# Normalised input laid out with features in rows: loaded turned from DRAM and normalised in place, in place of transposes on TensorE

## The chip, the cores and the metric

The kernel runs on one core of one Trainium2 chip. The metric is the device time of one execution in microseconds; the time before is the median of three runs. A core has engines with a queue each, which work in order and wait for each other by semaphores: PE (TensorE, matrix products into PSUM), DVE (VectorE), ACT (ScalarE), POOL (GpSimd) and SP, which here issues DMAs. PEld is PE's loading of weights.

## The reference

A residual block on x of 8 sequences of 512 tokens with 256 features: layer norm, then windowed attention (16 heads of 16, each token sees the last 250) and a gated feed-forward net with weights of +1 and -1, multiplied.

```python
def _layernorm(x, axis=-1, eps=1e-05):
    m = jnp.mean(x, axis=axis, keepdims=True)
    v = jnp.var(x, axis=axis, keepdims=True)
    return (x - m) / jnp.sqrt(v + eps)
...
    x = L0_attn_query
    xn = _layernorm(x, axis=-1)
    s = _L0_attn_ref(xn, L0_attn_in_proj_w, L0_attn_out_proj_w)
    g = _silu(_L0_ffn_ref(xn, L0_ffn_k0, L0_ffn_k1, L0_ffn_k2, L0_ffn_s0, L0_ffn_s1, L0_ffn_s2))
    x = x + s * g
```

In attention q, k and v are xn times the rows of in_proj_w, q and k are rotated by position, and softmax runs over the window. In the net, h = relu(s0 * [xn, -xn] @ w0) * 2, h = relu(s1 * h @ w1) * 2, h = s2 * h @ w2, with 1024 hidden columns twice.

## The kernel before

**Layout.** A sequence is four tiles of 128 tokens (rows) by 256 features. Layer norm wants tokens in rows, so that mean and variance run along a row; the products of q, k, v and the net want features in rows, because PE contracts over rows. So each tile is normalised (`norm`, DVE, line 250) and then turned by PE: `turn_x` (line 268) multiplies two 128x128 blocks by an identity into PSUM (`xnT_ps`). From PSUM come three things: `xT` in fp32 (DVE line 280, ACT line 278 for sequence 0), its high part `xh` in fp16 with a factor of 128 and the sign of s0 (ACT, line 281), and the rest `xl` (DVE, line 284). The net runs over high and low parts, so each product is done twice (`layer`, line 415: h1 from x in 8 column blocks, h2 from h1 in 8; `last`, line 441: z).

**Stages of a sequence b.** `stats` (DVE, with the power -1/2 on POOL, line 240), `norm`, `turn_x`, then `project` (PE, line 307: ka, kb, qa, qb, the even and odd members of the rotation pairs), times cos and sin on DVE (line 319), `rotate` on POOL (line 339), splits into two parts (ACT 356, DVE 363), a trip through DRAM that stacks heads (`to_dram`, `stack`, on SP), `scores`, exponentials (ACT 624), masks (POOL 640 and 647), `values` into po, divisions, `project_o` (line 782), the product with the gate, and the residual. `project_v` (line 292) is done at the start of the sequence itself. Preparation of sequence b+1 runs beside the net and the attention of b.

**Order.** All of it is written as pieces (time, cost, function) and one function `run` sorts them by time and calls them; a piece can return followers with a delay. The times are the planner's own, in which a sequence is SEQ = 42 long, against some 75 us on the chip; they set nothing but the order of instructions in the engines' queues. The order among engines is kept by semaphores.

**Buffers.** `one` holds a single xT, xh and xl. PSUM pool `ps_m` has three banks in rotation for h, z, q/k/v, att and xnT; `ps_s` two for scores, `ps_o` one for values. `turned` holds m_ka, m_kb and their like: tag `ma` twice, tag `mb` once. `work` holds two each of xn, den and xr.

**Start and end.** While the first x is loaded and normalised, `warm` has PE multiply the identity 16 times. The weights w1 arrive as bytes and are turned to +1 and -1 with a scale by POOL (line 180) and ACT (line 178), block by block, among other work. In the last sequence h2 runs in two halves of 256 tokens, and for its tiles 2 and 3 `project_o` comes before `last`: att goes to SBUF on ACT (line 791) and the end (lines 450 to 464) is exponential, plus 1, reciprocal, product and sum on DVE, then the store.

```python
at = dict(stats=9 if b > 1 else 12, norm=14.5, x=16.5, k=22, q=25, v=SEQ + 0.6)
...
out += [
    (at["norm"] + dx * t, 0, lambda t=t: norm(b, t)),
    (at["x"] + dx * t, 0.25, lambda t=t: turn_x(b, t, plain)),
    (at["v"] + dv * t, 0.87, lambda t=t: project_v(b, t)),
]
```

Of the kernel before, what the change touches and what calls it, by code (L numbers as in the profile page):

```python
# [11 lines left out]
F32 = mybir.dt.float32  # L12
F32R = mybir.dt.float32r
# [21 lines left out]
def tile_attention_times_gated_ffn(  # L35
    ctx: ExitStack,
    tc: tile.TileContext,
    x: bass.AP,
    w_qkv: bass.AP,
    w_o: bass.AP,  # L40
    k0: bass.AP,
# [3 lines left out]
    rope: bass.AP,  # L45
    out: bass.AP,
):

# [152 lines left out]

    quick = set()

    def warm():

        pw = ps_m.tile([P, P], F32, tag="mm", name="warm")
        for n in range(16):
            nc.tensor.matmul(pw, ident, ident, start=(n == 0), stop=(n == 15))  # L210

    def run(pieces):
        clock, count_, due = 0.0, itertools.count(), []
# [17 lines left out]
    def stats(b):  # L231
        st = states[b] = {}
        mv = small.tile([P, NT, 2], F32, tag="mv", name=f"mv_{b}")
        rstd = small.tile([P, NT], F32, tag="rstd", name=f"rstd_{b}")
        for t in range(NT):
            bn = small.tile([P, 6], F32, tag="bn", name=f"bn_{b}_{t}")
            nc.vector.bn_stats(bn, xs[b, t])
            nc.vector.bn_aggr(mv[:, t, :], bn)
        nc.vector.tensor_scalar(rstd, mv[:, :, 1], EPS, None, ALU.add)
        nc.gpsimd.tensor_tensor(rstd, rstd, minus_half, ALU.pow)  # L240
        nc.vector.scalar_tensor_tensor(
            mv[:, :, 1], mv[:, :, 1], LEAST_VAR, ones, ALU.is_ge, ALU.mult,
            accum_out=counts[:, 2 * B + b : 2 * B + b + 1],
        )
        st["mv"], st["rstd"] = mv, rstd

    def norm(b, t):
        st = states[b]
        xn = st["xn", t] = work.tile([P, E], F32, tag="xn", name=f"xn_{b}_{t}")
        nc.vector.tensor_scalar(  # L250
            xn, xs[b, t], st["mv"][:, t, 0:1], st["rstd"][:, t : t + 1],
            ALU.subtract, ALU.mult,
        )

    def turn_x(b, t, plain=False):

        st = states[b]
        xn = st.pop(("xn", t))
        if t == 0:
            st["xT"] = one.tile([P, EC, T], F32, tag="xT", name=f"xT_{b}")  # L260
            if plain:
                st["xp"] = one.tile([P, EC, T], F32, tag="xl", name=f"xp_{b}")
            else:
                for p, dt in (("h", F16), ("l", F32R)):
                    st["x" + p] = one.tile([P, EC, T], dt, tag="x" + p, name=f"x{p}_{b}")
        pt = ps_m.tile([P, EC, P], F32, tag="mm", name=f"xnT_ps_{b}_{t}")
        for c in range(EC):
            nc.tensor.transpose(pt[:, c, :], xn[:, ts(c, P)], ident)  # L268
        if plain:
            nc.vector.tensor_copy(st["xT"][:, :, ts(t, P)], pt)  # L270
            nc.scalar.mul(st["xp"][:, :, ts(t, P)], pt, sgnx)
            return
        hi, lo = (st["x" + p][:, :, ts(t, P)] for p in "hl")

        def parts_():
            xT = st["xT"][:, :, ts(t, P)]
            if b == 0:
                nc.scalar.copy(xT, pt)
            else:
                nc.vector.tensor_copy(xT, pt)  # L280
            nc.scalar.mul(hi, pt, sgnx)

        def low():
            nc.vector.scalar_tensor_tensor(lo, pt, sgnx, hi, ALU.mult, ALU.subtract)

        return [(0.0, parts_), (0.5, low)]
# [15 lines left out]
    def project(b, what, part):  # L302
        st = states[b]
        col = E * "qk".index(what) + P * "ab".index(part)
        ps = ps_m.tile([P, T], F32, tag="mm", name=f"{what}{part}_ps_{b}")
        for c in range(EC):
            nc.tensor.matmul(  # L307
                ps, wqkv_sb[:, c, ds(col, P)], st["xT"][:, c, :],
                start=(c == 0), stop=(c == EC - 1),
            )  # L310

        m = turned.tile(
            [P, 2, T], F32, tag=f"m{part}", name=f"m_{what}{part}_{b}",
            bufs=2 if part == "a" else 1,
        )
        st[what, part] = m

        def times(i):
            nc.vector.tensor_tensor(  # L319
                m[:, i], ps, rope_sb[:, i if part == "a" else 1 - i], ALU.mult  # L320
            )

        def both():
            times(0)
            times(1)
            if part == "b":
                return [
                    (1.4, lambda: rotate(b, what)),
                    (4.0 if b else 7.0, lambda: split_hi(b, what)),
                    (5.1 if b else 8.2, lambda: split_lo(b, what)),  # L330
                ]

        return [(0.0, both)]
# [39 lines left out]

    def prepare(b, plain=False):

        if b == 0:
            at = dict(stats=-40, norm=-38, x=-36, k=0, q=3, v=9.2)
            dx, dp, dv = 1.0, 1.5, 1.5
        else:

            at = dict(stats=9 if b > 1 else 12, norm=14.5, x=16.5, k=22, q=25, v=SEQ + 0.6)
            dx, dp, dv = 1.5, 1.5, 1.0
            at = {n: SEQ * (b - 1) + f for n, f in at.items()}
        out = [(at["stats"], 0, lambda: stats(b))]
        for t in range(NT):
            out += [
                (at["norm"] + dx * t, 0, lambda t=t: norm(b, t)),
                (at["x"] + dx * t, 0.25, lambda t=t: turn_x(b, t, plain)),
                (at["v"] + dv * t, 0.87, lambda t=t: project_v(b, t)),
            ]  # L390
        for what in "kq":
            out += [
                (at[what], 1.75, lambda w=what: project(b, w, "a")),
                (at[what] + dp, 1.75, lambda w=what: project(b, w, "b")),
            ]
        return out
# [32 lines left out]
    def last(b, t, how):  # L429
# [16 lines left out]
        if how == "final":  # L446
            den = denominator(b, t)

            def ends():
                nc.scalar.activation(den, pz, AF.Exp, scale=scales[:, 1:2])  # L450
                nc.vector.scalar_tensor_tensor(
                    gate, pz, scales[:, 0:1], st["att", t], ALU.mult, ALU.mult
                )
                return [(0.5, add)]

            def add():
                nc.scalar.activation(den, den, AF.Identity, bias=1.0)
                return [(0.4, final)]

            def final():  # L460
                nc.vector.reciprocal(den, den)
                nc.vector.tensor_tensor(gate, gate, den, ALU.mult)
                nc.vector.tensor_tensor(gate, gate, st["xr", t], ALU.add)
                nc.sync.dma_start(out[b, ts(t, P), :], gate)

            return [(0.0, ends)]

        def scale():
            nc.vector.tensor_scalar(gate, pz, scales[:, 0:1], None, ALU.mult)
            if how != "later":  # L470
                return [(0.5, lambda: gate_ready(b, t))]

        return [(0.0, scale)]

# [45 lines left out]

    def late(b, t):

        if b + 1 == B:
            return SEQ * b + 40.0 + 0.9 * t
        return SEQ * (b + 1) + (32.0 + 3.2 * t if b + 2 < B else 18.0 + 2.5 * t)
# [194 lines left out]
    def attention(b, among):  # L720
# [16 lines left out]
            out.append((times[n], 1.7, lambda n=n: step(b, n)))  # L737
        for g in range(NG):

            at = times[used[g - 2][-1]] + 0.01 if g > 1 else first - (10.0 if b else 2.0)  # L740
            if b and g == 1:
                at = first + 0.01
            out.append((at, 0, lambda g=g: stack(b, g)))
# [34 lines left out]
    def project_o(b, t, final=False):  # L778
# [7 lines left out]
        xr = work.tile([P, E], F32, tag="xr", name=f"xr_{b}_{t}")  # L786
        nc.sync.dma_start(xr, x[b, ts(t, P), :])
        st["xr", t] = xr
        if final:
            att = st["att", t] = work.tile([P, E], F32, tag="xn", name=f"att_{b}_{t}")  # L790
            return [(0.0, lambda: nc.scalar.copy(att, pp))]

        def product():
            y = st["gate", t]
            nc.vector.tensor_tensor(y, pp, y, ALU.mult)
            return [(0.5, store)]

        def store():
            y = st.pop(("gate", t))
# [35 lines left out]
    def swap():  # L835
# [2 lines left out]
        outs = ctx.enter_context(tc.tile_pool(name="outs", bufs=1))  # L838

    everything = [  # L840
        (-38.5, 0, signs), (-40.5, 0, warm),
        (18.2, 0, make_w2), (22.5, 0, swap), (SEQ * (B - 1) + 45.0, 0, add_up),
    ]
    for c in range(EC):
        everything.append((-30 + 0.1 * c, 0, lambda c=c: make_w0(c)))
    for w, f, at, engine in (
        ("l", 0, -20, nc.gpsimd), ("l", 1, -19, nc.gpsimd), ("l", 2, -18, nc.gpsimd),
        ("h", 0, -17, nc.scalar), ("h", 1, -16, nc.scalar), ("h", 2, 5, nc.gpsimd),
        ("l", 3, 9.0, nc.gpsimd), ("l", 4, 9.1, nc.gpsimd), ("l", 5, 9.2, nc.gpsimd),
        ("l", 6, 9.3, nc.gpsimd), ("l", 7, 9.4, nc.gpsimd), ("h", 3, 15.2, nc.scalar),  # L850
        ("h", 4, 17.0, nc.scalar), ("h", 5, 18.7, nc.scalar), ("h", 6, 20.4, nc.scalar),
        ("h", 7, 22.2, nc.scalar),
    ):
        everything.append((at, 0, lambda f=f, w=w, e=engine: make_w1(f, w, e)))
# [139 lines left out]
```

## Time and profile before

| | us |
|---|---|
| median of 3 runs | 631.65 (629.59 to 631.93) |
| profiled execution | 632.4 |
| its span, first to last instruction | 630.6 |
| PE busy in it | 609.6 |
| DVE, POOL, ACT busy | 393.0, 316.1, 300.0 |
| transposes, PE, 64 of 285 ns (overlapping) | 12.8 |
| xn, xl, xT on DVE | 23.3, 15.1, 11.7 |
| xh on ACT | 15.3 |

The page lists busy time by engine and groups of instructions by line and tile. [...]sums of lengths overstate, and start to start is what counts. The mean granted TensorE clock was 0.993. Between the span and the execution's time lie 1.8 us.

### The profile page before, as it was taken

What the parts mean: (1) busy time and instruction counts of PE and PEld (TensorE: products, weight loads), DVE (VectorE), ACT (ScalarE), POOL (GpSimd) and SP (SyncE); (2) the same over time, 40 slices, a digit from 0 to 9 for tenths busy, and PEclk for the clock granted to TensorE, in tenths of its full rate; (3) what the DMA queues carried; (4) which work ended last, traced back from release to release, by engine and by line L of the source; (5) the groups of instructions that cost most, each with busy time, mean ns of one, the idle gap of its engine ahead of it and who ended that gap; (6) DMA issues with size and microseconds to landing.
All of it is one profiled execution on the core that took longest, in us unless ns stands there. A gap on an engine that the chain in (4) does not pass through costs nothing.

```text
span 630.6 us, 12029 instructions
## 1 busy us (share of the span) xinstructions
PE 609.6 (97%) x4834; PEld 398.8 (63%) x4834; DVE 393.0 (62%) x668; ACT 300.0 (48%) x442; POOL 316.1 (50%) x406
## 2 busy tenths in 40 slices
PE   7899999999999999999999999999999999999993
PEld 5454566656665567755676566765676556777883
DVE  6582545757656674766758576485675668457664
ACT  3566564525455445535355454453444544564421
POOL 1945452356623566327644367234662356638630
PEclk9899999999999999999999999999999999999998
DMA  8261821125321163113521153402532116230101
GB/s 269 81 234 51 300 86 50 36 83 210 101 76 50 68 223 112 51 51 144 166 93 51 55 221 96 132 25 94 207 107 73 51 68 226 76 109 18 53 26 40
DMA packets 38193, 67.20 MB, mean 107 GB/s; under 512 B 5104, under 2 KB 19184, under 8 KB 38128
## 3 DMA queue, kind: packets, MB, share of 16 engines
q1 hardware_dynamic: 36384, 64.24, 30.2%
q10 hardware_dynamic: 1744, 2.10, 1.0%
q8 instruction: 40, 0.66, 0.4%
q14 instruction: 25, 0.20, 0.1%
HBM read 36.96 MB, written 29.36 MB: 105 GB/s over the span
## 4 chain that ended last, share of the span: by engine, by line
PE 84%; DVE 6%; DMA 4%; POOL 3%; ACT 2%; issue 1%; SPq 0%; POOLq 0%; ACTq 0%
PE h_ps L415 40%; PE po L679 11%; PE z_ps L441 9%; PE sc L605 7%; PE v_ps L292 4%; PE att_ps L782 4%; PE qa_ps L307 2%; PE kb_ps L307 2%; PE qb_ps L307 2%; DMA kb<-in_k_dram 2%; DMA xr<-in_x_dram 2%; PE ka_ps L307 2%; PE xnT_ps L268 1%; DVE den L505 1%; ACT p L624 1%
## 5 line engine op out<-in xcount | busy, mean ns | idle before, releaser
L624 ACT ACTIVATE p<-sc 128x1024 f32<-128x1024 f32 (+2 forms) x144 | 138.5, 1013 | 75.0 <-PE sc L605 41.0
L640 POOL TENSOR_SCALAR_AFFINE_SELECT p<-p 128x512 f32<-128x512 f32 x128 | 93.8, 739 | 106.5 <-ACT p L624 106.5
L415 PE MATMUL h_ps<-h1l,w1l_sb 128*128 128x512 f32 (+1 forms) x576 | 144.2, 392 | 0.0
L415 PE MATMUL h_ps<-h1h,w1h_sb 128*128 128x512 f16 (+1 forms) x576 | 123.0, 356 | 0.9 <-ACT v_pad L299 0.5
L415 PEld LDWEIGHTS h_ps<-h1l,w1l_sb 128*128 128x128 f32 x576 | 99.5, 188 | 25.7 <-issue 6.8
L426 ACT ACTIVATE h2h<-h_ps 128x512 f16<-128x512 f32 (+1 forms) x72 | 39.6, 550 | 136.5 <-PE h_ps L415 136.4
L415 PEld LDWEIGHTS <-w1h_sb 128*128 128x128 f16 x576 | 51.6, 98 | 55.8 <-issue 14.0
L647 POOL TENSOR_SCALAR_AFFINE_SELECT p<-p 128x512 f32<-128x512 f32 (+1 forms) x96 | 50.4, 525 | 58.0 <-ACT p L624 56.7
L679 PE MATMUL po<-p,v_pad 128*32 128x378 f32 (+4 forms) x1216 | 77.0, 372 | 1.6 <-DVE S L703 1.1
L424 DVE SCALAR_TENSOR_TENSOR h2l<-h_ps,h2h 128x512 fp32r<-128x512 f32 (+1 forms) x72 | 44.4, 617 | 52.0 <-ACT h2h L426 52.0
L505 DVE RECIPROCAL den<-den 128x256 f32<-128x256 f32 x30 | 52.5, 1749 | 26.0 <-POOL den L501 26.0
L424 DVE SCALAR_TENSOR_TENSOR h1l<-h_ps,h1h 128x512 fp32r<-128x512 f32 x64 | 42.5, 675 | 36.1 <-ACT h1h L426 36.1
L605 PEld LDWEIGHTS sc<-q,k 32*128 32x128 f32 x1216 | 44.1, 184 | 26.1 <-issue 15.0
L754 DVE RECIPROCAL S<-S 128x128 f32<-128x128 f32 x64 | 58.9, 934 | 0.0
L426 ACT ACTIVATE h1h<-h_ps 128x512 f16<-128x512 f32 x64 | 38.2, 597 | 43.0 <-PE h_ps L415 42.8
L605 PE MATMUL sc<-q,k 32*128 32x378 f32 (+4 forms) x1216 | 57.3, 306 | 0.0
L415 PE MATMUL h_ps<-xl,w0l_sb 128*128 128x512 f32 x128 | 53.6, 500 | 0.0
L679 PEld LDWEIGHTS po<-p,v_pad 128*32 128x32 f32 x1216 | 31.5, 109 | 30.8 <-issue 16.6
L800 POOL TENSOR_TENSOR gate<-gate,xr 128x256 f32<-128x256 f32 x30 | 23.1, 770 | 46.7 <-DMA xr<-in_x_dram 32.6
L415 PE MATMUL h_ps<-xh,w0h_sb 128*128 128x512 f16 x128 | 39.5, 391 | 0.1
L441 PE MATMUL z_ps<-w2l_sb,h2l 128*128 128x256 f32 x256 | 38.1, 291 | 0.0
L339 POOL TENSOR_TENSOR m_ka<-m_ka,m_kb 128x512 f32<-128x512 f32 x16 | 20.1, 1276 | 30.3 <-DVE m_kb L319 30.3
(95 smaller groups left out, 806.6 us busy)
## 6 DMA issues: line engine op xcount, KB each, us to landing
q<-dq SPq DMA_DIRECT2D x64, 256.0 KB, 3.5
dq<-qh SPq DMA_DIRECT2D x16, 512.0 KB, 3.4
dq<-m_qa SPq DMA_DIRECT2D x16, 512.0 KB, 4.6
k<-dk SPq DMA_DIRECT2D x32, 256.0 KB, 2.8
dk<-kh SPq DMA_DIRECT2D x8, 512.0 KB, 2.7
dk<-m_ka SPq DMA_DIRECT2D x8, 512.0 KB, 2.7
xr<-in_x_dram SPq DMA_DIRECT2D x32, 128.0 KB, 2.3
out_dram<-gate SPq DMA_DIRECT2D x32, 128.0 KB, 1.7
```

Source lines behind the costliest of these rows:

```text
L307: nc.tensor.matmul(ps, wqkv_sb[:, c, ds(col, P)], st["xT"][:, c, :], start=(c == 0), stop=(c == EC - 1),)
L415: nc.tensor.matmul(ph, w[p][:, c, ts(f, P)], st[src + p][:, c, cols], start=(k == 0), stop=(k == n - 1),)
L424: nc.vector.scalar_tensor_tensor(lo, ph, 0.0, hi, ALU.max, ALU.subtract)
L426: high = lambda: nc.scalar.activation(hi, ph, AF.Relu)
L441: nc.tensor.matmul(pz, st["h2" + p][:, c, ts(t, P)], w2[p][:, c], start=(c == 0 and p == "h"), stop=(c == NF1 - 1 and p == "l"),)
L505: nc.vector.reciprocal(den, den)
L605: nc.tensor.matmul(sc[r // 2][:, r % 2, ds(off, n)], st["k0", g][row, ts(j, P)], st[f"q{turn}", g][row, ds(j * P + first, n)], start=(turn ...
L624: nc.scalar.activation(p[:, 2 * half : 2 * half + 2, :n], sc[half][:, :, :n], AF.Exp, scale=D ** -0.5,)
L640: nc.gpsimd.affine_select(out=block, in_=block, compare_op=ALU.is_ge, fill=0.0, base=0, pattern=[[0, 4], [1, P]], channel_multiplier=-1,)
L647: nc.gpsimd.affine_select(out=block, in_=block, compare_op=ALU.is_ge, fill=0.0, base=-1, pattern=[[0, 4], [-1, beyond]], channel_multiplier=1,
L679: nc.tensor.matmul(po[32 * r : 32 * r + 32, ds(j * P + first, n)], v_columns(j, g, r), p_[:, r, ds(off, n)], start=(j == 0), stop=(done an ...
L754: nc.vector.reciprocal(part, part)
```

## The change

The host also passes x with features and tokens exchanged (`x_t`). For sequences 1 to 7 this is loaded straight into xT (`load_xT`). `stats` still runs on tiles with tokens in rows, and puts means and inverse deviations side by side (`both`, 4 + 4 values a row). `lay_over` writes them to DRAM in the order of tokens and reads them back so that every row has all 512 means and 512 deviations (`of_all`, in the place of an m_kb). `norm_turned` subtracts and multiplies in place on DVE, for each half of the features, and makes xh (ACT) and xl (DVE) from SBUF. Sequence 0 keeps the old way, and so does the fallback path behind the check of ranges.

The times of pieces move: sequence 1's projections and stacks, POOL's w1 blocks, two of the splits in sequence 0, and `warm` (12, 3 and 5 products among the transposes, in `ps_o`). At the end `project_o` of tiles 2 and 3 comes after the last `last`, and their products are shared out over POOL, DVE and ACT.

```diff
-    def warm():
-
-        pw = ps_m.tile([P, P], F32, tag="mm", name="warm")
-        for n in range(16):
-            nc.tensor.matmul(pw, ident, ident, start=(n == 0), stop=(n == 15))
+    def warm(count_):
+
+        pw = ps_o.tile([P, P], F32, tag="po", name="warm")
+        for n in range(count_):
+            nc.tensor.matmul(pw, ident, ident, start=(n == 0), stop=(n == count_ - 1))
...
-        rstd = small.tile([P, NT], F32, tag="rstd", name=f"rstd_{b}")
+        both = small.tile([P, 2, NT], F32, tag="both", name=f"mean_rstd_{b}")
+        rstd = both[:, 1]
...
+        nc.vector.tensor_copy(both[:, 0], mv[:, :, 0])
+        st["both"] = both
+
+    raw_xT = {}
+
+    def load_xT(b):
+        raw_xT[b] = one.tile([P, EC, T], F32, tag="xT", name=f"xT_{b}")
+        nc.sync.dma_start(raw_xT[b], x_t[b].rearrange("(c p) t -> p c t", p=P))
+
+    def lay_over(b):
+
+        st = states[b]
+        d = dram.tile([2, NT, P], F32, tag="both", name=f"d_both_{b}")
+        nc.sync.dma_start(d.rearrange("i t p -> p i t"), st["both"])
+        of_all = st["of_all"] = turned.tile(
+            [P, 2, T], F32, tag="mb", name=f"of_all_{b}", bufs=1
+        )
+        nc.sync.dma_start(of_all, d.rearrange("i t p -> i (t p)").partition_broadcast(P))
+
+    def norm_turned(b, c):
+
+        st = states[b]
+        if c == 0:
+            st["xT"] = raw_xT.pop(b)
...
+        xT = st["xT"][:, c]
+        for i, op in enumerate((ALU.subtract, ALU.mult)):
+            nc.vector.tensor_tensor(xT, xT, st["of_all"][:, i], op)
+        hi, lo = (st["x" + p][:, c] for p in "hl")
+
+        def low():
+            nc.vector.scalar_tensor_tensor(lo, xT, sgnx, hi, ALU.mult, ALU.subtract)
+
+        return [(0.8, lambda: nc.scalar.mul(hi, xT, sgnx)), (1.3, low)]
...
-                    (4.0 if b else 7.0, lambda: split_hi(b, what)),
-                    (5.1 if b else 8.2, lambda: split_lo(b, what)),
+                    (4.0 if b else 5.5, lambda: split_hi(b, what)),
+                    (5.1 if b else 6.3, lambda: split_lo(b, what)),
...
-            at = dict(stats=9 if b > 1 else 12, norm=14.5, x=16.5, k=22, q=25, v=SEQ + 0.6)
-            dx, dp, dv = 1.5, 1.5, 1.0
+            at = dict(load=6, stats=9, over=11, norm=16.8, k=21.8, q=24.8, v=SEQ + 0.6)
+            if b == 1:
+                at.update(load=14.8, stats=12, over=18.8, norm=23, k=27, q=29)
+            dp, dv = 1.5, 1.0
...
+        if "over" in at:
+            out += [
+                (at["load"], 0, lambda: load_xT(b)), (at["over"], 0, lambda: lay_over(b)),
+                (at["norm"], 0, lambda: norm_turned(b, 0)),
+                (at["norm"] + 1.2, 0, lambda: norm_turned(b, 1)),
+            ]
...
-                nc.vector.scalar_tensor_tensor(
-                    gate, pz, scales[:, 0:1], st["att", t], ALU.mult, ALU.mult
-                )
-                return [(0.5, add)]
+                nc.vector.tensor_scalar(gate, pz, scales[:, 0:1], None, ALU.mult)
+                return [(0.3, add)]
...
-            def final():
+            def invert_():
                 nc.vector.reciprocal(den, den)
-                nc.vector.tensor_tensor(gate, gate, den, ALU.mult)
-                nc.vector.tensor_tensor(gate, gate, st["xr", t], ALU.add)
-                nc.sync.dma_start(out[b, ts(t, P), :], gate)
+                if t + 1 < NT:
+                    nc.gpsimd.tensor_tensor(gate, gate, den, ALU.mult)
+                st["den"] = den
...
-                return [(0.5, lambda: gate_ready(b, t))]
+                return [(0.5 if t == 0 else 4.5, lambda: gate_ready(b, t))]
...
+        if b + 1 == B and t >= NT // 2:
+            return last_at(b, NT - 1) + L3 + 0.9 * (t - NT // 2)
...
-            at = times[used[g - 2][-1]] + 0.01 if g > 1 else first - (10.0 if b else 2.0)
+            at = times[used[g - 2][-1]] + 0.01 if g > 1 else first - (5.0 if b == 0 else 4.0 if b == 1 else 9.0)
...
+            def out_of_psum():
+                y, den = st["gate", t], st["den"]
+                nc.scalar.copy(att, pp)
+                nc.gpsimd.tensor_tensor(y, y, att, ALU.mult)
+                nc.vector.tensor_tensor(y, y, den, ALU.mult)
+                nc.vector.tensor_tensor(y, y, xr, ALU.add)
+                nc.sync.dma_start(out[b, ts(t, P), :], y)
...
-        (-38.5, 0, signs), (-40.5, 0, warm),
-        (18.2, 0, make_w2), (22.5, 0, swap), (SEQ * (B - 1) + 45.0, 0, add_up),
+        (-38.5, 0, signs), (-40.5, 0, lambda: warm(12)), (-34.5, 0, lambda: warm(3)),
+        (-32.5, 0, lambda: warm(5)),
+        (19.2, 0, make_w2), (22.5, 0, swap), (SEQ * (B - 1) + 45.0, 0, add_up),
...
-        ("l", 0, -20, nc.gpsimd), ("l", 1, -19, nc.gpsimd), ("l", 2, -18, nc.gpsimd),
-        ("h", 0, -17, nc.scalar), ("h", 1, -16, nc.scalar), ("h", 2, 5, nc.gpsimd),
-        ("l", 3, 9.0, nc.gpsimd), ("l", 4, 9.1, nc.gpsimd), ("l", 5, 9.2, nc.gpsimd),
-        ("l", 6, 9.3, nc.gpsimd), ("l", 7, 9.4, nc.gpsimd), ("h", 3, 15.2, nc.scalar),
+        ("l", 0, -20, nc.gpsimd), ("l", 1, -19, nc.gpsimd), ("l", 2, 5.1, nc.gpsimd),
+        ("h", 0, -17, nc.scalar), ("h", 1, -16, nc.scalar), ("h", 2, 5.2, nc.gpsimd),
+        ("l", 3, 11.8, nc.gpsimd), ("l", 4, 11.9, nc.gpsimd), ("l", 5, 12.0, nc.gpsimd),
+        ("l", 6, 19.3, nc.gpsimd), ("l", 7, 19.4, nc.gpsimd), ("h", 3, 15.2, nc.scalar),
...
         "x": x,
+        "x_t": x.transpose(0, 2, 1),
```

## The prediction

> **What bounds the kernel now.** I read the page's busy times and the chain that ended last first, to learn which engine the time belongs to; then the timeline of PE in one sequence in the middle, to price what is removed; then start and end, where PE is not the bound.
>
> ```profile
> PE 609.6 (97%) x4834; PEld 398.8 (63%) x4834; DVE 393.0 (62%) x668; ACT 300.0 (48%) x442; POOL 316.1 (50%) x406
> ...
> PE 84%; DVE 6%; DMA 4%; POOL 3%; ACT 2%; issue 1%; SPq 0%; POOLq 0%; ACTq 0%
> ```
>
> PE is busy 97% of the span and 84% of the chain; no other engine passes 62%. In the middle of the run the time is PE's, so an instruction taken out of PE's queue there is worth what PE spends on it, and work moved to DVE, ACT or DMA costs nothing until PE waits for it.
>
> ```profile
> 339.01 1.90 PE L415 MATMUL h_ps<-h1h,w1h_sb 128*128 128x512 f16 x8
> 340.56 2.20 PE L415 MATMUL h_ps<-h1l,w1l_sb 128*128 128x512 f32 x8
> 342.60 0.38 PE L268 MATMUL xnT_ps<-ident,xn 128*128 128x128 f32 x2
> 342.82 1.89 PE L415 MATMUL h_ps<-h1h,w1h_sb 128*128 128x512 f16 x8
> 344.80 0.89 PE L268 MATMUL xnT_ps<-ident,xn 128*128 128x128 f32 x4
> 345.45 2.12 PE L415 MATMUL h_ps<-h1l,w1l_sb 128*128 128x512 f32 x8
> 347.40 0.38 PE L268 MATMUL xnT_ps<-ident,xn 128*128 128x128 f32 x2
> 347.71 0.74 PE L605 MATMUL sc<-q,k 32*128 32x256 f32 x16
> ...
> 309.90 1.90 PE L415 MATMUL h_ps<-h1h,w1h_sb 128*128 128x512 f16 x8
> 311.45 2.20 PE L415 MATMUL h_ps<-h1l,w1l_sb 128*128 128x512 f32 x8
> 313.48 1.02 PE L782 MATMUL att_ps<-wo_sb,V 128*128 128x256 f32 x4
> ```
>
> Columns are start, length, instruction. Matmuls overlap, so cost is read from start to start. The second rows show one undisturbed h2 column block: 309.90 to 313.48, 3.58 us (3.59 in the first rows, 339.01 to 342.60; 3.68 where scores follow, 292.93 to 296.61). The first rows show two blocks with all four tile transposes of the next sequence: 339.01 to 347.71, 8.70 us.
>
> ```profile
> 22.00 1.29 DVE L319 TENSOR_TENSOR m_qb<-qb_ps,rope_sb 128x512 f32<-128x512 f32 x2 [3.20 <-POOL m_ka L339]
> ...
> 23.35 1.16 PE L292 MATMUL v_ps<-wqkv_sb,xT 128*128 128x256 f32 x4 [2.33 <-DVE m_qb L319]
> ...
> 25.00:30.00 5.00, 5.00 (x18) 3.06 (x18) 2.53 (x3) 2.80 (x5) 5.00 (x4) 0.73 0.28 112
> ...
> 622.51 1.74 DVE L461 RECIPROCAL den<-den 128x256 f32<-128x256 f32 x1
> ...
> 624.75 0.42 DVE L463 TENSOR_TENSOR gate<-gate,xr 128x256 f32<-128x256 f32 x1
> ```
>
> The start has the only long stall of PE after its first transpose: v_ps waits for DVE, which waits for POOL's rotation of m_ka (brackets give the wait), and the granted clock then falls to 0.73. At the end PE's last z matmul starts at 619.12, but DVE still works alone until 625.17.
>
> [...] The write of means and deviations has 1,024 elements of 4 bytes; this trace has no such write of data. [...]
>
> **The change, part by part.**
>
> 1. *Transposes.* In PE's compiled order 28 of the 32 tile pairs are gone, those of sequences 1 to 7; sequence 0 keeps its four. Two bare blocks cost 3.59 + 3.68 = 7.27, against 8.70: 1.43 us each for sequences 2 to 7 (the six stretches read 8.69 to 8.71), 8.6 together. For sequence 1 the stretch is 35.82 to 43.92 and 44.65 to 44.92, 8.37: 1.10. Sum 9.7. Bounds: 28 bare pairs at 0.22 (342.60 to 342.82) are 6.2; 7 times 1.43 is 10.0.
>
> 2. *DVE and ACT.* Out per sequence: xn 4 x 0.752, xT copies 4 x 0.418, xl 4 x 0.475, 6.6 us of DVE; xh 4 x 0.479 of ACT. In: four tensor_tensors of 128x512, two xl and two xh of 128x512, one tiny copy. No row shows the tensor_tensor from SBUF at this size; 128x256 took 0.424 and the PSUM form 0.686. The nearest row in size gives 0.69[...]. With 0.68 for each xl and 0.2 for the copy: 4.3 us. DVE loses 2.3 us per sequence; hidden under PE, worth nothing.
>
> 3. *The round trip through DRAM,* the part that can lose. I lay it over the sequence above. rstd leaves POOL at 337.28 + 1.05 = 338.33. SP's queue then holds only the group-2 stacks, already issued by 332, so the write goes at 338.4. Its price is unknown: an output store of 128 KB lands in 1.7[...]; I take 2.5 (bounds 1.7 and 7). The broadcast is 512 KB in long rows, like dk<-kh, 2.7. of_all lands at 338.4 + 2.5 + 0.2 + 2.7 = 343.8. DVE, in order, sits before its first subtraction from 340.4. Behind it: h2l of block 0, the count of R, later h2l; behind xh on ACT: h2h of block 1 and the exponentials of step 4. Then two tensor_tensors to 345.2, h2l 345.9, xl 346.5 (xh has run on ACT meanwhile), two tensor_tensors: both halves of xT ready at 347.8[...]. PE wants it at ka: blocks 0 and 1 end at 339.01 + 7.27 = 346.28, the scores and values take 2.31 (347.71 to 350.02), the next h1h 1.73 (350.02 to 351.75): 350.3. Slack 2.5 us, so I price the wait at nothing. The PSUM ring of three also holds: ka needs h2l of block 0, out at 345.9. The exponentials of step 4 end near 351, their masks at 352.9; their values run near 356.5. If this cover fails, each microsecond beyond it costs 6 us over the steady sequences.
>
> On SP, the write and the broadcast stand ahead of the group-3 stacks, which wait for PE's scores until 348.27 anyway. The load of x_t (512 KB) waits for the previous v_ps (over at 323.4) and lands ten microseconds before use; behind it stand the group-2 stacks, issued at 331 anyway: nothing.
>
> 4. *Start.* POOL makes two w1l blocks, not three, before rotating m_ka: 3.56 / 3 = 1.2 earlier, so m_qb starts at 20.8 and v_ps at 22.15. The stall halves, which may spare the low clock too (worth 5 x 0.07 + 5 x 0.27 = 1.7 us, from 0.93 granted between 20 and 25 us and 0.73 after). But DVE is then next: its statistics of sequence 1 take 2.6 (30.95 to 33.5) with another 1.2 of m_qa now ahead of h1l_4. Walking DVE's order I get h1l_5 at 31.6, h1l_6 at 32.2, and the first h2 block at 33.8 for 35.82. The warm matmuls between transposes stand in gaps of 0.2 and 0.5 and could delay ka by 0.3; ACT's copies end at 11.4 and set it now. I take 2.0; bounds -0.5 and 4. In sequence 0 SP's x_t load stands ahead of the first stacks: 1.28 MB at about 300 GB/s from the end of v_ps is 4.3 + 1.5, against 7.7 to the first scores.
>
> 5. *End.* att for tiles 2 and 3 move behind z: z ends 2 x 0.87 = 1.7 earlier, PE ends when it did (620.3). DVE then runs gate and reciprocal of tile 2 (to 619.4), of tile 3 (to 621.5), the att_2 product, and two tensor_tensors of tile 3 (0.43 each) to 622.8; POOL has multiplied gate_3 by att_3 at 621.5. SP issues tile 3's store, then tile 2's at 623.15 instead of 625.2: 2.0. Bounds 0.5 and 2.6.
>
> Sum: 9.7 + 2.0 + 2.0 = 13.7. The profiled execution took 632.4 (span 630.6); it would be 618.7, its span 616.9. The median shown, 631.65, is 0.75 lower than that execution: 631.65 - 13.7 = 618.0.
>
> **Rivals.**
>
> - *The round trip comes late* by about a microsecond: element-wise writes are unlike anything in the trace. For it: DVE visibly has to wait for of_all even by my walk. Against: 2.5 us of slack. Six sequences at 1.0: 624.
> - *Slower:* the same place, before ka of each next sequence, with the element-wise write taking 7 us or more beyond my 2.5. It decides from 13.7 / 6 = 2.3 us past the slack, a write of 2.5 + 2.5 + 2.3 = 7.3 us. At 9 us the six pay 4.0 each, 24: 642. Against: 20-byte rows (s_sb, 128 of them) land in 5.8 even in the crowded start.
> - *Start and end give nothing:* the warm matmuls push ka, the x_t load pushes the first stacks, POOL's and ACT's hand-offs at the end eat what z gains. 9.7 remains: 622.
> - *The change doesn't do what it says:* excluded for the transposes by the compiled order; the same matmuls otherwise remain.
>
> **How the numbers follow.** 0.68 for 618, 0.13 for late by one, 0.09 for the slower case, 0.10 for start and end giving nothing. The range 613.5 to 625.5 takes the likeliest with its bounds (PE's 10.0 and the upper ends of start and end make 614) and the two middle cases; what is left out is mostly the slow case. Half a per cent is 3.2 us, about what a measurement of this kernel can tell from no change. Faster by more than that: the likeliest and most of the two middle cases, 0.86; within it, a round trip late by two, 0.05; slower 0.09.
>
> **What would show it.** In the changed kernel two h2 blocks start to start should take about 7.3 us up to step 4's scores, and ka should show no wait on DVE's xT. DVE's first subtraction should wait on a DMA by some 3 us. The first h2 block should start near 33.8, and about 2 us should lie between the last reciprocal and the last store's issue. A PE wait on xT in every sequence, or a landing of the 4-byte write above 5 us, would make the forecast wrong.

## The result, and the profile after

The changed kernel takes 679.49 us (median of 4 runs, 678.36 to 681.69) against 630.78 of the kernel before, run beside it: a ratio of 1.077, 95% interval 1.0753 to 1.0788. It is slower by 48.7 us where 13.7 us less were forecast. The profiled execution took 680.1 us with a span of 678.3.

From the page of the kernel after: busy times, the granted clock in forty slices, and the chain of waits by engine.

```profile
PE 619.5 (91%) x4786; PEld 397.7 (59%) x4786; DVE 384.6 (57%) x633; ACT 294.9 (43%) x427; POOL 317.4 (47%) x409
...
PEclk9997999979999899989999799997999979999998
...
PE 60%; DMA 21%; DVE 9%; POOL 3%; ACT 2%; issue 2%; SPq 1%; POOLq 0%; ACTq 0%; DVEq 0%
```

PE has 48 matmuls less and is busy 10 us longer: the slices with a 7, and those with an 8 before the last, hold stretches at a lower clock, one for each of the seven sequences. DMA, 4% of the chain before, is 21%.

The waits of the kernel after (engine, line, what it waited for, us in total, times, longest):

```profile
DVE xT L279 <- DMA of_all<-d_both: 90.4, 7, 14.3
...
PE ka_ps L344 <- DVE h2l L470: 32.3, 6, 6.4
```

DVE waits for `of_all` in all seven sequences, 12.9 us on average; PE waits for DVE before ka. The releaser named is `h2l`, not `xT`: DVE works in order (xT at 382.36, h2l at 383.69 in the rows below), and the h2l whose PSUM bank ka needs stands behind the subtraction that waits. These are six stalls of 4.8 to 6.4 us, in sequences 2 to 7. In sequence 1 the stall, of 5.7 us, stands before scores and is put down to ACT: its exponentials stand behind an xh that waits 8.6 us for xT.

The DMA issues of the kernel after (size, median us from issue to landing):

```profile
of_all<-d_both SPq DMA_DIRECT2D x7, 512.0 KB, 4.8
...
d_both<-mean_rstd SPq DMA_DIRECT2D x7, 4.0 KB, 10.8
```

The 4 KB need longer, 10.8 us, than the 512 KB, 4.8. One steady sequence in the timeline of the kernel after shows the whole of it (start, length, instruction, the wait ahead of it in brackets):

```profile
367.27 0.37 SPq L264 DMA_DIRECT2D d_both<-mean_rstd  x1
...
367.93 1.90 PE L461 MATMUL h_ps<-h1h,w1h_sb 128*128 128x512 f16 x8
...
375.20 0.74 PE L651 MATMUL sc<-q,k 32*128 32x256 f32 x16
...
376.40 0.32 SPq L268 DMA_DIRECT2D of_all<-d_both  x1
...
382.36 1.42 DVE L279 TENSOR_TENSOR xT<-xT,of_all 128x512 f32<-128x512 f32 x2 [12.94 <-DMA of_all<-d_both]
383.69 0.68 DVE L470 SCALAR_TENSOR_TENSOR h2l<-h_ps,h2h 128x512 fp32r<-128x512 f32 x1
...
384.43 2.08 PE L344 MATMUL ka_ps<-xT,wqkv_sb 128*128 128x512 f32 x2 [5.02 <-DVE h2l L470]
```

The two h2 blocks take 375.20 - 367.93 = 7.27 us, as forecast for bare ones. But SP can issue the broadcast only 9.1 us after the write, DVE starts 6.0 us later, and PE has stood still for 5.02 us when ka starts. PE wanted ka at 384.43 - 5.02 = 379.4.

The windows of the kernel after before and around that stall (stretch, length, PE busy, granted clock, DMA share, GB/s):

```profile
370.00:376.40 6.40, 6.40 (x48) 1.00 0.00 0
...
376.00:384.00 8.00, 3.40 (x32) 0.92 0.57 164
382.00:383.00 1.00, 0.00 (x0) 0.89 1.04 401
384.00:391.00 7.00, 6.38 (x13) 0.60 0.00 0
389.00:390.00 1.00, 1.00 (x5) 0.69 0.00 0
391.00:400.00 9.00, 9.00 (x49) 1.00 0.24 92
```

The first row is the time in which the write has been issued and hasn't landed: the profile counts no packet on any DMA engine (share 0.00). In the six steady sequences the share is 0.17 to 0.22 in the first 2.7 us after the write's issue, and 0.03 or less from then until the broadcast goes out. So the packets of the slow write are soon over; what takes the rest of its time isn't in the trace.

The clock lacks 8 x 0.08 + 7 x 0.40 = 3.4 us' worth, which is half rate for 6.8 us, from about 382.8 to 389.6: in every microsecond from 383 to 389 the granted clock is 0.50. The part before 384.43 costs nothing, since PE stands. From ka's start to qb's PE then takes 397.46 - 384.43 = 13.03 us, and 10.13 in e1_rows below, which has no stall (417.97 to 428.10): 2.9 us more, 0.2 of it a second short wait for xT. A sequence thus loses 5.0 + 2.9 = 7.9 us.

The starts of qb's matmuls give nearly the same. Two neighbouring sequences of the kernel before, of the kernel after and of e1_rows:

```profile
361.89 1.88 PE L307 MATMUL qb_ps<-xT,wqkv_sb 128*128 128x512 f32 x4
436.79 1.88 PE L307 MATMUL qb_ps<-xT,wqkv_sb 128*128 128x512 f32 x4
...
315.74 1.88 PE L344 MATMUL qb_ps<-xT,wqkv_sb 128*128 128x512 f32 x4
397.46 1.88 PE L344 MATMUL qb_ps<-xT,wqkv_sb 128*128 128x512 f32 x4
...
428.10 1.88 PE L346 MATMUL qb_ps<-xT,wqkv_sb 128*128 128x512 f32 x4
501.53 1.88 PE L346 MATMUL qb_ps<-xT,wqkv_sb 128*128 128x512 f32 x4
```

It is 74.90 us from sequence to sequence before, 81.72 after, and 73.43 where nothing stalls: 8.3 us for a stall. Seven make 58 us, which is what separates this kernel from e1_rows (679.49 - 621.22 = 58.3).

### The profile page after: what moved, and what is told of

Its sections match the earlier page's. It is cut to its first block, busy times and chain, and to the rows that moved or that the text cites. A ratio compares the mean times of both kernels' runs of the same rounds, so it can differ in the third digit from the quotient of the medians.

```text
span 678.3 us, 11932 instructions
## 1 busy us (share of the span) xinstructions
PE 619.5 (91%) x4786; PEld 397.7 (59%) x4786; DVE 384.6 (57%) x633; ACT 294.9 (43%) x427; POOL 317.4 (47%) x409
## 2 busy tenths in 40 slices
DMA packets 48384, 74.55 MB, mean 110 GB/s; under 512 B 12608, under 2 KB 26688, under 8 KB 48320
## 4 chain that ended last, share of the span: by engine, by line
PE 60%; DMA 21%; DVE 9%; POOL 3%; ACT 2%; issue 2%; SPq 1%; POOLq 0%; ACTq 0%; DVEq 0%
PE h_ps L461 26%; DMA d_both<-mean_rstd 9%; PE po L725 8%; PE z_ps L487 7%; PE sc L651 5%; PE v_ps L329 4%; DMA of_all<-d_both 4%; DMA xr<-in_x_dram 3%; PE att_ps L828 3%; DVE xT L279 2%; PE ka_ps L344 2%; DMA q<-dq 2%; PE qb_ps L344 2%; PE qa_ps L344 2%; PE kb_ps L344 2%; DMA kb<-in_k_dram 2%
## 5 line engine op out<-in xcount | busy, mean ns | idle before, releaser
L461 PE MATMUL h_ps<-h1l,w1l_sb 128*128 128x512 f32 (+1 forms) x576 | 150.4, 404 | 0.0
L461 PEld LDWEIGHTS h_ps<-h1l,w1l_sb 128*128 128x128 f32 x576 | 103.4, 194 | 30.5 <-issue 9.7
L693 POOL TENSOR_SCALAR_AFFINE_SELECT p<-p 128x512 f32<-128x512 f32 (+1 forms) x96 | 49.0, 511 | 63.1 <-ACT p L670 60.6
L279 DVE TENSOR_TENSOR xT<-xT,of_all 128x512 f32<-128x512 f32 x28 | 19.3, 689 | 90.8 <-DMA of_all<-d_both 90.4
L651 PEld LDWEIGHTS sc<-q,k 32*128 32x128 f32 x1216 | 44.7, 186 | 34.9 <-issue 16.8
L344 PE MATMUL ka_ps<-xT,wqkv_sb 128*128 128x512 f32 x32 | 28.9, 1013 | 33.5 <-DVE h2l L470 32.3
L285 ACT ACTIVATE xh<-xT,sgnx 128x512 f16<-128x512 f32 x14 | 10.1, 722 | 93.1 <-DVE xT L279 69.5
```

The lines of the kernel that those rows point to most:

```text
L344: nc.tensor.matmul(ps, wqkv_sb[:, c, ds(col, P)], st["xT"][:, c, :], start=(c == 0), stop=(c == EC - 1),)
L461: nc.tensor.matmul(ph, w[p][:, c, ts(f, P)], st[src + p][:, c, cols], start=(k == 0), stop=(k == n - 1),)
L651: nc.tensor.matmul(sc[r // 2][:, r % 2, ds(off, n)], st["k0", g][row, ts(j, P)], st[f"q{turn}", g][row, ds(j * P + first, n)], start=(turn ...
L693: nc.gpsimd.affine_select(out=block, in_=block, compare_op=ALU.is_ge, fill=0.0, base=-1, pattern=[[0, 4], [-1, beyond]], channel_multiplier=1,
```

## The experiments

**What is late: the write, its pieces, or the broadcast?** The theory (A): the 1,024 elements of 4 bytes make the write late. Rivals: any small write that is read back is so slow (B), the broadcast is late (C), or the rows' arithmetic and the edits at start and end cost something (D).

*e1_rows:*

```diff
-        d = dram.tile([2, NT, P], F32, ...)
-        nc.sync.dma_start(d.rearrange("i t p -> p i t"), st["both"])
+        d = dram.tile([P, NT, 2], F32, ...)
+        nc.sync.dma_start(d, st["both"])
...
-            nc.vector.tensor_tensor(xT, xT, st["of_all"][:, i], op)
+            of_t = st["of_all"][:, :, :, i].rearrange("q p t -> q t p")
+            x3 = xT.rearrange("q (t p) -> q t p", p=P)
+            nc.vector.tensor_tensor(x3, x3, of_t, op)
```

> The 4 KB of means and deviations are written as 128 pieces of 32 bytes, one contiguous row of each partition, where the changed kernel writes 1,024 pieces of 4 bytes; the broadcast reads the same 4 KB, and DVE reads its rows with a stride. Nothing else moves. Theory A (the 1,024 small elements make the write late): from its issue to the issue of the broadcast 3 to 4 us instead of 9.1, of_all lands about 9 us after the write's issue instead of 15.1, which is inside the 10.0 us that PE leaves (ka was wanted at 379.4, DVE needs 2.1, the write went at 367.3); no wait of PE on DVE before ka, the time 617 to 622. Rival B (any small write that is read back through DRAM is that slow, whatever its pieces): the 9.1 us stay and so do 679. Rival C (the broadcast is what is late): of_all still lands some 12 us or more after the write's issue, the time above 640.

Measured: 621.22 us, ratio 0.985 (0.983 to 0.9871): 1.5% faster than the kernel before. Its DMA issues and, below, one steady sequence of its timeline:

```profile
of_all<-d_both SPq DMA_DIRECT2D x7, 512.0 KB, 3.6
...
d_both<-mean_rstd SPq DMA_DIRECT2D x7, 4.0 KB, 1.4
```

```profile
406.00 0.32 SPq L264 DMA_DIRECT2D d_both<-mean_rstd  x1
407.44 0.32 SPq L268 DMA_DIRECT2D of_all<-d_both  x1
411.19 2.67 DVE L281 TENSOR_TENSOR xT<-xT,of_all 128x512 f32<-128x512 f32 x2 [3.04 <-DMA of_all<-d_both]
...
417.97 1.88 PE L346 MATMUL ka_ps<-xT,wqkv_sb 128*128 128x512 f32 x4
```

The same 4 KB in 128 rows land in 1.4 us instead of 10.8. DVE still waits, 3.0 us, as step 3 of the prediction had it, and ka starts with no wait. Reading with a stride makes each tensor_tensor 1.2 us on average instead of 0.69; PE doesn't feel it. A holds against B and C, and D falls.

*e2_no_dep:*

```diff
-        nc.sync.dma_start(of_all, d.rearrange("i t p -> i (t p)").partition_broadcast(P))
+        nc.sync.dma_start(of_all, rope[0, 7:9, :].partition_broadcast(P))
```

> The write of 1,024 elements stays in its place, but the broadcast reads 4 KB of the rope table and so doesn't wait for it; this changes what x is normalised with (a cosine row for the mean, another for the deviation), so the values are others and the work is the same. Theory A and rival B both say: of_all lands 5 to 6 us after the stats, PE has no wait before ka, 617 to 622. Rival C (the broadcast itself, 128 readers of one 4 KB region, sets the time): PE still waits, well above 640. Rival D (the late landing is only part, and normalising on DVE in long rows or the edits at start and end cost something of their own): no wait on the DMA, yet more than 624.

Measured: 677.31 us, ratio 1.073 (1.0705 to 1.0754), which no theory on the list had expected except C, and C's reading is wrong too, since the same broadcast lands in 3.6 us in e1_rows. One steady sequence of e2_no_dep:

```profile
364.32 0.37 SPq L264 DMA_DIRECT2D d_both<-mean_rstd  x1
364.74 2.18 SPq L268 DMA_DIRECT2D of_all<-in_rope_dram  x1
...
379.55 1.42 DVE L279 TENSOR_TENSOR xT<-xT,of_all 128x512 f32<-128x512 f32 x2 [13.08 <-DMA of_all<-in_rope_dram]
381.63 2.08 PE L344 MATMUL ka_ps<-xT,wqkv_sb 128*128 128x512 f32 x2 [5.17 <-DVE h2l L470]
```

The broadcast needs none of the write's data, goes out 0.4 us behind it and still arrives 14.8 us later. So the write is not only late itself: it holds up what is issued behind it. The contrast is f4_spread below, where the same broadcast behind a quick write lands in 5.0.

*e4_early* splits `lay_over`; load, statistics and write come one sequence ahead, in sequence 1 only the write:

```diff
-            at = dict(load=6, stats=9, over=11, ...)
+            at = dict(load=6, stats=9 - SEQ, out=11 - SEQ, over=8, ...)
-                at.update(load=14.8, stats=12, over=18.8, norm=23, k=27, q=29)
+                at.update(load=14.8, stats=12, out=13, over=18.8, norm=23, k=27, q=29)
+            if b == 2:
+                at.update(stats=30 - SEQ, out=32 - SEQ)
```

> The same 1,024-element write, made early: from sequence 2 on the statistics and the write are due one sequence ahead (x is loaded ahead for that), the broadcast then waits for nothing that is late; in sequence 1 the write alone is issued before the loads and stacks that stood ahead of it. Theory A: the landing is as slow as before but nobody waits; the steady sequences lose their stall and the low clock behind it, sequence 1 keeps a smaller one: 617 to 622, about 12 less than the kernel before. Rival D (normalising in rows costs more than the transposes): above 628. If the write disturbs other transfers by its 1,024 elements, and not by being waited for, the time stays above 640.

Measured: 637.08 us, ratio 1.01 (1.0077 to 1.0124), outside all that was expected. From sequence 2 on it is 73.4 to 74.3 us from qb to qb, as A says. What remains is at the start: qb of sequence 2 comes at 148.90, 15.4 us later than in e1_rows, of 16.8 in the whole span. Its timeline there:

```profile
32.45 0.37 SPq L263 DMA_DIRECT2D d_both<-mean_rstd  x1
33.43 0.38 SPq L258 DMA_DIRECT2D xT<-in_x_t_dram  x1
33.91 0.42 SPq L412 DMA_DIRECT2D k<-dk  x1
34.42 0.86 SPq L412 DMA_DIRECT2D q<-dq  x2
...
48.44 1.70 PE L658 MATMUL sc<-q,k 32*128 32x378 f32 x16 [7.86 <-DMA q<-dq]
```

The first stacks, moved behind the write, are now the held transfers, and PE waits 7.86 us for them. A write that nobody waits for still costs by what stands behind it.

**Does it hold its queue (E) or what all queues share (F)?** *f1_no_dep_act* and *f2_act*, from e2_no_dep and from the changed kernel:

```diff
-        nc.sync.dma_start(d.rearrange("i t p -> p i t"), st["both"])
+        nc.scalar.dma_start(d.rearrange("i t p -> p i t"), st["both"])
```

> As e2_no_dep (the broadcast reads rope rows and waits for no data of the write, so the values are others), but the write of 1,024 elements is issued on ACT's queue. In e2_no_dep the broadcast stood right behind the write on SP's queue and landed 14.8 us after its issue though it waited for nothing. Theory E (a write in small elements holds the queue that it is on, whoever waits for it): the broadcast lands 3 to 5 us after its issue, no wait of PE before ka, 618 to 622. Rival F (it holds the DMA engines[...]): the broadcast still needs 10 us or more, about 677.

> The changed kernel with only the write moved to ACT's queue; the broadcast waits for its data as before and the result is the same. The write's own landing should stay 9 to 12 us whatever the queue, so of_all lands some 13 to 15 us after the write's issue and PE still waits: 670 to 680. If the slowness belongs to SP's queue or to what stands in it, the write lands in 2 to 4 us and the time is about 620.

f1_no_dep_act: 623.68 us (0.987 to 0.9903). It looks like E, but tells little: in the steady sequences SP issued the broadcast up to 6 us before ACT got to the write (330.31 and 336.27). Only in sequence 1 did it go behind, and there it was held:

```profile
37.33 0.38 ACTq L264 DMA_DIRECT2D d_both<-mean_rstd  x1
37.60 0.33 SPq L268 DMA_DIRECT2D of_all<-in_rope_dram  x1
48.90 1.42 DVE L279 TENSOR_TENSOR xT<-xT,of_all 128x512 f32<-128x512 f32 x2 [6.73 <-DMA of_all<-in_rope_dram]
```

f2_act: 672.08 us, ratio 1.0663 (1.0643 to 1.0683); the write lands in 10.0 us on ACT's queue too. *g3_two_queues* settles the order that f1_no_dep_act left loose:

```diff
+        nc.scalar.copy(after_pow, st["both"][:, 1])
-        nc.sync.dma_start(of_all, rope[0, 7:9, :].partition_broadcast(P))
+        nc.scalar.dma_start(of_all, rope[0, 7:9, :].partition_broadcast(P))
```

> As e2_no_dep (no dependency, other values), the write on SP's queue, the broadcast on ACT's queue and held back there until the deviations are ready, so that it is issued right after the write. In f1_no_dep_act the broadcast went 6 us ahead of the write in the steady sequences and told nothing; in sequence 1, where it went 0.3 us after it on the other queue, it landed after 11.2 us. If the write holds the queue alone (E): the broadcast lands in 4 to 6 us, 620 to 624. If it holds what all queues share (F): 10 us and more, 665 to 680.

Its DMA issues:

```profile
of_all<-in_rope_dram ACTq DMA_DIRECT2D x7, 512.0 KB, 10.8
...
d_both<-mean_rstd SPq DMA_DIRECT2D x7, 4.0 KB, 12.7
```

Measured: the broadcast, issued in six of the seven sequences 0.07 us behind the write on the other queue, lands in 10.8 us (9.0 to 12.5). That is what F said of the landing. No run has a broadcast on ACT's queue beside a quick write; but in sequence 1 of f1_no_dep_act, with the queues exchanged, it took 11.2. The time, 639.48 us (ratio 1.0114 to 1.0161), is below F's 665: a landing of 10 us lies just at what PE leaves, so PE stands for 1.6 to 2.6 us at the first wait before ka in three of the six steady sequences and for 0.4 to 1.0 in the others. What the two queues share isn't shown, nor that the DMA engines are what is held: in the changed kernel they carry no packet for most of the write's time (share 0.00 from 370.00 to 376.40).

**Number of pieces, or where they fall?** *e5_eights* (512 pieces of 8 bytes) and *f4_spread* (from e2_no_dep, each element in 64 bytes of its own):

```diff
+        d = dram.tile([NT, P, 2], F32, ...)
+        nc.sync.dma_start(d.rearrange("t p i -> p t i"), st["both"])
...
+        d = dram.tile([2, NT, P, 16], F32, ...)
+        nc.sync.dma_start(d[:, :, :, 0].rearrange("i t p -> p i t"), st["both"])
```

> Mean and deviation of a row are written side by side: 512 pieces of 8 bytes instead of 1,024 of 4; the broadcast reads the same 4 KB and DVE reads it with a stride of two. If the cost goes with the number of pieces: 9.1 us between the issues for 1,024 and 1.4 us for the landing of 128 rows of 32 bytes give about 4.7 us for 512; of_all then lands about 9.5 us after the write, just inside the 10.0 us: 620 to 630. If any write below some size is equally slow: about 9 us again and 670 to 680.

> As e2_no_dep (write and broadcast both on SP's queue, no dependency, other values), but each of the 1,024 elements goes to a 64-byte line of its own in DRAM, so no two of them share a line. If the number of elements is what costs, nothing changes: the broadcast lands about 15 us after its issue, 677. If it is that neighbouring elements, 4 bytes apart, meet in the same line, the write lands in 2 to 4 us, the broadcast in 4 to 7, and the time is 618 to 625.

e5_eights: 621.9 us (0.982 to 0.9891), the write in 4.0. f4_spread: 619.78 us (0.98 to 0.9833), the write in 3.5. My own theory, that the number of pieces costs, falls with f4_spread: it sends 1,024 elements, and its page counts the same 12,608 packets under 512 bytes as the changed kernel's. What is left is where they fall. *g1_pitch8* is f4_spread with `[2, NT, P, 2]`, so that elements stand 8 bytes apart; *g2_one_owner* writes e1_rows' layout out of an SBUF tile with gaps, so that 2 partitions share 64 bytes and not 16:

> As f4_spread (1,024 elements of 4 bytes, broadcast of rope rows right behind on the same queue, no dependency, other values), but the elements stand 8 bytes apart in DRAM, 8 in each 64 bytes, where f4_spread has 1 and the changed kernel 16. Theory G (pieces that fall into the same 64 bytes are what is slow, the more the slower): between the two, the write landing at 4 to 9 us against 3.5 and 12.1. Rival H (only elements that touch each other are slow): as f4_spread, 3 to 4 us, 620.

> As e1_rows in DRAM (the 8 values of one partition side by side in 32 bytes, read back with a stride), but sent as 1,024 separate elements of 4 bytes, since the values stand 8 bytes apart in SBUF. Each 64 bytes take 16 elements as in the changed kernel, now from 2 partitions where there they come from 16. If the elements of 4 bytes in shared 64 bytes are slow whoever sends them (G): 9 to 12 us between the two issues and 670 to 680. If it matters that 16 partitions meet in the same 64 bytes, the write lands in 2 to 5 us and the time is 620 to 626.

g1_pitch8: 619.21 us (0.9799 to 0.9833), the write in 5.1. g2_one_owner: 680.76 us (1.0772 to 1.0811), the write in 7.9 (6.8 to 12.4), a little below the 9 to 12 expected: elements in the same 64 bytes stay slow when 2 partitions send them and not 16, by 3 us less. The last three ask whether it is touching in the same 8 bytes, many in 64, or many at all. *h1_pairs_touch* and *h2_pairs_apart* write means to place 0 and deviations to place 1 or 2 of each row of `[NT, P, 16]`, in two transfers; *h3_half* writes `d[0]` from `st["both"][:, 0]` alone:

> As f4_spread (no dependency, the broadcast reads rope rows behind the write, other values), the write now as two transfers of 512 elements: the mean of a row at the start of a 64-byte line, its deviation in the 4 bytes after it. If elements in the same 8 bytes are what is slow: the broadcast lands about 14 us after its issue, 670 to 680. If it takes many elements in one 64 bytes: landing 4 to 6 us as in f4_spread, 619 to 622.

> As h1_pairs_touch, but the deviation stands 8 bytes after the mean, in the same 64 bytes. Under both theories fast: landing 4 to 6 us, 619 to 622. If this one is slow as well, any two elements in one line are enough when they come from two transfers, and h1_pairs_touch tells nothing of the 8 bytes.

> As e2_no_dep (no dependency, other values), but only the means are written: 512 elements of 4 bytes side by side, 16 in each 64 bytes as in the changed kernel; the deviations are left out of the write. If the time goes with the number of such elements: about half of 12.1, so a landing of the write at 6 to 7, of the broadcast at 7.5 to 9, just inside what PE leaves: 620 to 630. If any such write is slow: 12 and 14.8 us, 677.

h1_pairs_touch 619.7 us (0.9762 to 0.9854), h2_pairs_apart 620.0 us (0.9768 to 0.9857), h3_half 653.36 us (1.0273 to 1.0408), between its two expectations. Touching pairs, in two transfers, are not slow; 512 elements side by side land in 10.3 us, hardly sooner than 1,024. By the pieces that share 64 bytes (a size that I chose to count in; no run shows that the chip counts so), with the median landing of the write:

| pieces in 64 bytes | kernel | pieces | landing, us |
|---|---|---|---|
| 1 | f4_spread | 1,024 of 4 bytes | 3.5 |
| 2 | h1_pairs_touch, h2_pairs_apart | 2 x 512 of 4 | 2.6, 2.4 |
| 2 | e1_rows | 128 of 32 | 1.4 |
| 8 | e5_eights | 512 of 8 | 4.0 |
| 8 | g1_pitch8 | 1,024 of 4 | 5.1 |
| 16 | h3_half | 512 of 4 | 10.3 |
| 16 | changed kernel, g2_one_owner, e2_no_dep, g3_two_queues | 1,024 of 4 | 10.8, 7.9, 12.1, 12.7 |

Two readings fit every row: many pieces in 64 bytes, or pieces of one transfer that touch, two in the same 8 bytes. All slow writes have both. g1_pitch8's step from 3.5 to 5.1 speaks for the first, but single landings of the two overlap (2.8 to 6.0 and 4.4 to 7.3), and h1_pairs_touch has its touching pieces in two transfers. No run has touching pieces of one transfer with few in 64 bytes, so this stays open.

The lines of the DMA issues behind two rows that differ in nothing but the distance, f4_spread first, then e2_no_dep:

```profile
of_all<-in_rope_dram SPq DMA_DIRECT2D x7, 512.0 KB, 5.0
...
d_both<-mean_rstd SPq DMA_DIRECT2D x7, 4.0 KB, 3.5
```

```profile
of_all<-in_rope_dram SPq DMA_DIRECT2D x7, 512.0 KB, 14.8
...
d_both<-mean_rstd SPq DMA_DIRECT2D x7, 4.0 KB, 12.1
```

**Start and end.** *e3_start_end* keeps the transposes with their times (`stats` 9 or 12, `norm` 14.5, `x` 16.5, `k` 22, `q` 25, xT copied by DVE, stacks as before) and has the rest of the change; *g4_prep_alone* is e1_rows with `warm`, the w1 list, splits, `late`, `last` and `project_o` of the kernel before.

> Only the edits at the start (order of the w1 blocks, warm matmuls, due times of the splits) and at the end (att of tiles 2 and 3 behind z, gate and att multiplied on POOL); the transposes and their due times are those of the kernel before, and no means go through DRAM. From the changed kernel's trace the start gains 1.15 us and the end about 1.45, so 2.6 less than before (ratio 0.996). My prediction had 4.0 (ratio 0.9937). Rival D: 0 or a loss.

> e1_rows (write in rows of 32 bytes) with the start and the end of the kernel before: order of the w1 blocks, warm matmuls, splits, att before z, all as they were. With 0.2 us for those edits from e3_start_end, this should be 621 to 622, the ratio 0.985. If they are worth the 2.6 us that the trace of the changed kernel shows, 623.8, a ratio of 0.989.

e3_start_end: 630.63 us, ratio 0.9999 (0.9988 to 1.001): nothing, to within 0.8 us. g4_prep_alone: 626.28 us, ratio 0.9942 (0.9923 to 0.996), about 5 us above e1_rows and outside both expectations. The same edits are worth nothing beside the transposes and 5 us beside the new layout. A part of why is in the granted clock: over its executions g4_prep_alone has 0.990 on average, e1_rows 0.997, which by my estimate is worth 0.0062 x 622 = 3.9 us. In the profiled execution v_ps waits 2.00 us at 22.96, against 1.52 in e1_rows. The rest isn't explained. Where in the span the other executions lost their clock isn't recorded.

## Why the prediction was wrong

**Step 3 failed, by its first term.** It took 2.5 us for the landing of the write, my estimate of 0.8 on top of the 1.7 of a 128 KB store, with bounds of 1.7 and 7. The upper bound had no row behind it: the only small pieces in that trace were one row for each partition, and the write's elements are of another kind. Measured, 10.8, and PE stood in all seven sequences; a landing above 5 us was the sign of being wrong that the prediction had named. It had named element-wise writing as the unknown, too. The pages show one packet for each piece: 12,608 packets under 512 bytes against 6,336 in e1_rows, a difference of 7 x (1,024 - 128). But one packet each is no price: 1,024 of them cost 3.5 us or 12.1, by where they fall.

**Its second term:** the broadcast was taken at 2.7. It landed in 4.8 behind the slow write, 3.6 behind a fast one. With rows of 32 bytes the two terms come to 1.4 + 3.6 = 5.0 us, against 5.2 in the prediction, for a write of another shape. DVE's wait, 3.0 us where some 3 were forecast, and the order were right; that the sum agrees is luck in part, since one term was 1.1 too long and the other 0.9 too short.

**The slack** was underestimated. From the write to DVE's start it was 15.1 us, 9.7 more than the 5.4 assumed, and PE stood for 5.0: the slack was 4.7, not 2.5.

**The slower rival** had the place and the mechanism. Its point of decision, a write of 7.3 us, is only bracketed, by runs whose broadcast waits for no data: h3_half's 10.3 loses 21 us, g1_pitch8's 5.1 nothing. At the measured 10.8 its rule gives 618.0 + 6 x (10.8 - 5.0) = 653. Most of the 27 us that are missing are the seventh stall and the 2.9 us of low clock behind each stall, a kind of loss that the prediction had priced at the start of the kernel and left out here.

**Step 1 was right.** Two blocks in 7.27 us; 74.90 us from sequence to sequence become 73.43 where nothing stalls, 1.47 each where 1.43 was forecast. e1_rows against e3_start_end, which differ by the layout and the times of its pieces: 630.63 - 621.22 = 9.4 us, forecast 9.7. With the old start and end, g4_prep_alone against the kernel before, it is only 630.59 - 626.28 = 4.3; the gain for each sequence is shown, the whole depends on steps 4 and 5. **Step 2 was right:** tensor_tensor took 0.689 us, forecast 0.69, and DVE's changes are hidden, up to e1_rows' strided reads.

**Steps 4 and 5** were added as 2.0 + 2.0, independent of the rest. They are not: 0.2 us with the transposes, about 5 with the layout. In the trace of the changed kernel the first h2 block starts at 34.67 for 35.82 (1.15), for a forecast 33.8. There DVE's m_ka split, beside POOL's rotation of m_qa, took 3.52 us; before, beside POOL's w1 blocks, 1.23; step 4 hadn't this in it. In e1_rows and e3_start_end it took 2.25, and the first h2 block starts at 33.14 and 33.38: in those traces step 4 gains more than its 2.0. At the end, in the changed kernel, 3.2 us lie between PE's last matmul and the issue of the last store (669.43 to 672.58) where it was 4.9 (620.31 to 625.2): 1.7 of step 5's 2.0. Why nothing of either is left in e3_start_end's median stays open. Also, the low clock after the v_ps stall was priced off one execution: that execution of the kernel before had a clock of 0.992 (0.993 on its page), its later ones 0.994 on average, which is about 1 us of 630.

## What to carry to other kernels

A few kilobytes that pass through DRAM are to be written as rows, and put in order by whoever reads them: here the reader's stride cost 0.5 us of hidden DVE time in each of four instructions, the scattered write 9 us of landing. Before a small transfer is called hidden, ask what stands behind it on any queue (here a broadcast, 14.8 us on the same queue and 10.8 on another instead of 5.0), and what stands behind its waiter on its engine (here h2l behind the subtraction, which had PE stand for 5.02 us). A bound for a cost that no row shows must come from a row, or be left open and tried first.

## What the hardware showed unexpectedly

- Elements of 4 bytes side by side in DRAM, 16 in 64 bytes, land 8 to 13 us after their issue (medians), though in the changed kernel's steady sequences hardly a packet is left after 2.7 (share 0.03 or less); the same number 8 or 64 bytes apart in 5.1 and 3.5. Half as many save little (10.3).
- While such a write is under way, a transfer that has nothing to do with it is held as well, on the same queue (14.8 us instead of 5.0) and on another (10.8). What it is that holds them wasn't tried.
- A stall of 5.0 us cost another 2.9, all but 0.2 of it through the clock: half rate for 6.8 us, of which 1.7 fell before PE resumed. The clock was back 5.2 us after PE resumed. At the start of the kernel before, the half rate lasted 3.4 us (24.3 to 27.7, clock 0.50), after a stall of 2.3. What sets how long it lasts wasn't tried.
